# Layer 1 of a four-layer image network: VectorE in source order, small pieces between blocks, lengths after the values

## The chip, the core and the metric

The kernel runs on one core of a Trainium2 chip. The core has TensorE (PE, matrix products), VectorE (DVE), ScalarE (ACT), GpSimd (POOL) and SyncE (SP), which here issues the transfers. The metric is the device time of one execution in microseconds; the number quoted is the median of several executions.

## The reference

The input is 4 images of 56 x 56 positions (3136 tokens) with 256 channels, in 32-bit floats. Four layers follow each other, each adding its result to its input after a group normalisation. Only layer 1 is touched. For each image it computes:

```
xn = x / max(norm(x), 1e-12)                 # per token
A  = xn diag(W_adj) xn^T ; A = exp(5 (A - rowmax)) with a zero diagonal
A  = A / rowsum
y  = rowsum(A) * (x W_aff^T + b_aff) - (A x) W_aff^T
y  = LayerNorm(y) * gamma + beta ; y = max(y, 0.01 y)
```

x is the group-normalised input, and W_adj enters through its diagonal. The kernel applies W_aff first (the values xw = x W_aff^T), so one product A xw serves, and a column of -1 beside xw gives the row sums in the same product. A is symmetric before the division by the row sum, so a block of it computed once serves its rows and its columns.

## The kernel before

Layer 1 splits the 3136 tokens of an image into 24 tiles of 128 (NB) and a rest of 64 (REST). Tokens are loaded in chunks of four tiles: chunks 0 to 5 (NC4 is 6), and chunk 6 for the rest.

**Preparing tokens** (`tokens`, L1337). For a chunk there is a list of steps. `load` reads x (512 KB), normalises its two channel halves with the group statistics (L939, VectorE) and squares the result (L1355, ScalarE). `lengths` sums squares by TensorE products with a column of ones (L1363), limits them (L1365, VectorE), takes the power -1/2 (L1366, GpSimd) and spreads them on a diagonal (L1367, GpSimd). `values` multiplies two tiles by W_aff (L1376), copied out by ScalarE or VectorE (L954, L952). `unit_length` broadcasts the inverse lengths by a product with that diagonal (L1384) and multiplies (L1386, VectorE) into xnT.

**The loop over units.** A unit is a row tile j with up to four column tiles first to last (a block is one pair of tiles). `scaled` (L1401, GpSimd) multiplies row tile j by W_adj. `logits` (L1408) makes the products, ScalarE the exponentials (L1411), and on the diagonal GpSimd clears the main diagonal (L1413). `transposed` turns the blocks by TensorE (L1478) and ScalarE copies them (L1481). `products` then does for each column tile i a product by column into one of two PSUM buffers ps_v (L1497), which VectorE adds to acc in SBUF (`add_up`, L1420, or a first copy, L1423), and a product by row (L1492), summed in the PSUM buffer ps_o of tile j. The rest of 64 tokens has units of its own (`rest_logits`, `rest_transposed`, `rest_products`, L1459 and L1463), two of which for the next image stand after row tiles 20 and 21 of the image before, the third after row tile 0.

**Finishing a tile.** When row tile j has all its columns, `finish` (L1519) adds ps_o and acc (L1527), divides (L1531, L1533), takes mean and variance (L1536, L1537, L1538), their power -1/2 on GpSimd (L1540), normalises on VectorE (L1541), multiplies by gamma and adds beta on GpSimd (L1542, L1543) and takes the maximum on VectorE (L1544). It returns `add`, which transposes the tile back (L1549) and adds it to the residual xr (L1557); with all 448 tokens of a residual piece there, the statistics for layer 2 are taken (L894) and the piece is stored (L1561).

**The order of the work.** Two lists set it. `small` holds pairs of a due block count and a step; `small_step` runs one due step, twice in each unit: ahead of the transposes, and between the next unit's logits and the products. The steps of a chunk are due 8 blocks after its load, an add 6 blocks after its finish. `replace` starts a chunk of the next image at a certain row tile, once the current image no longer needs that chunk. `now` forces the steps of a chunk that a unit is about to read. The product order is written out like this because for layer 1 TensorE is fixed in source order (`run(1, ..., {E.PE}, ...)`). The instructions of the other engines and the transfers are put in order by a planner, which takes an instruction when its model says that it is ready, preferring earlier ones; the resulting order of each engine's queue is then static. Layers 0 and 2 are left to the planner wholly.

Of the kernel before, what the change touches and what calls it, by code (L numbers as in the profile page):

```python
# [35 lines left out]
P = 128  # L36
# [4 lines left out]
NCH = 7  # L41
# [789 lines left out]
def direct_blocks(ctx: ExitStack, tc: tile.TileContext, d: dict, watch):  # L831
# [488 lines left out]
    def layer1(early, big, pool, late, next_layer):  # L1320
# [16 lines left out]
        def tokens(b, c, ps_a=ps_m):  # L1337
# [6 lines left out]
            def load():  # L1344
                x = early.tile([P, CC, 512], FP, tag="x", name="x1")
# [5 lines left out]
                x1 = box["x"] = early.tile([P, CC, 512], FP, tag="xn", name="xn1")  # L1351
                sq = box["sq"] = x
                for h in range(CC):
                    normalise(x1[:, h, :n], x[:, h, :n], known(1, b), h)
                nc.scalar.activation(sq[:, :, :n], x1[:, :, :n], AF.Square)  # L1355

            def lengths():
                pm, sq = ps_a(), box["sq"]
# [33 lines left out]
            return [load, lengths] + [lambda i=i: values(i) for i in range(0, m, 2)] + [unit_length]  # L1392
# [23 lines left out]
        touched = set()  # L1416
# [36 lines left out]
        def rest_products(b, q, e, own, at):  # L1453
            po = psum_tile("o", 2)
            for i in range(4):
# [6 lines left out]
                for a in range(2):  # L1462
                    nc.tensor.matmul(po[a * REST:(a + 1) * REST, :C + 1], lhsT=at[:, i * P + a * REST:i * P + (a + 1) * REST],  # L1463
                                     rhs=xw[:, 8 * q + 4 * a + i, :], start=(i == 0), stop=(i == 3 and (a == 1 or own is None)))
            if own is not None:
# [18 lines left out]
        def products(b, j, first, last, e, at):  # L1484
# [18 lines left out]
            for n, i in enumerate(others):  # L1503
                by_column(i)
                if n:
                    by_row(rows.pop(0))
            for i in rows:
# [4 lines left out]
        def residual(b, c):  # L1512

            if (b, c) not in xr and c < NCH:
                xr[b, c] = late.tile([P, CC, CH], FP, tag="xr", name="xr1", bufs=3)
# [3 lines left out]
        def finish(b, j):  # L1519

            n = P if j < NB else REST
            y = late.tile([P, C + 1], FP, tag="y", name="y", bufs=5) if j < NB else y_rest
# [12 lines left out]
            mv = pool.tile([P, 2], FP, tag="mv", name="mv1")  # L1535
# [3 lines left out]
            rstd = pool.tile([P, 1], FP, tag="rstd", name="rstd")  # L1539
            nc.gpsimd.tensor_tensor(rstd[:n], mv[:n, 1:2], mhalf[:n, 0:1], ALU.pow)  # L1540
            nc.vector.tensor_scalar(y, y, mv[:n, 0:1], rstd[:n], ALU.subtract, ALU.mult)  # L1541
            nc.gpsimd.tensor_tensor(y, y, gamma[:n], ALU.mult)  # L1542
            nc.gpsimd.tensor_tensor(y, y, beta[:n], ALU.add)  # L1543
            nc.vector.scalar_tensor_tensor(y, y, 0.01, y, ALU.mult, ALU.max)  # L1544

            def add():
# [5 lines left out]
                while t0 < j * P + n:  # L1552
# [9 lines left out]
                    t0 = t1  # L1562
            return add
# [16 lines left out]
        for c in range(2):  # L1580
            fresh[c].pop(0)()
        for c in range(NC4 + 1):
            for step in fresh[c]:
                step()
            if c + 2 <= NC4:
                fresh[c + 2].pop(0)()
        small, done = [], 0

# [610 lines left out]
```

## Time and profile before

| | |
|---|---|
| runs shown | 4041.41, 4027.03, 4025.71 us, median 4027.03 |
| profiled execution | 4042.54 us, of which the span from first to last instruction is 4040.7 |
| TensorE busy | 3848.9 us (95%) |
| VectorE, ScalarE, GpSimd busy | 2356.6 (58%), 1381.2 (34%), 1746.3 us (43%) |
| mean granted TensorE clock | 0.974 |
| layer 1 on TensorE | from 811.0 us (first L1363) to 2813.4 us (last L1492) |

Line numbers are those of the kernel before. A stretch such as 860:2815 is in us from the start of the span. Busy time of TensorE alone doesn't tell a full clock from a half one; the column PEclk does. A wait is put down to the instruction that released it, by engine, tile and line.

### The profile page before, as it was taken

Reading aid. Unit: us, or ns where it says so; the run is one execution under the profiler, and the core shown is the slowest. Engines: PE = TensorE matmul, PEld = TensorE weight load, DVE = VectorE, ACT = ScalarE, POOL = GpSimd, SP = SyncE. Lnnn points to the kernel's source line nnn. Section 1 sums busy time; section 2 is a strip of 40 time slices with the busy share of each in tenths; the row PEclk is TensorE's granted clock in tenths of the full one; section 3 lists DMA queues with packets and bytes.
Section 4 is the critical chain, followed back from the end, with each engine's and each line's share of the span. In section 5 each row is a group of like instructions: output and inputs, shape, how many; then the busy total and the mean of one; then the engine's idle time right before and its main releaser. Section 6 shows DMA issues by size and latency. Waiting matters only on the chain.

```text
span 4040.7 us, 92344 instructions
## 1 busy us (share of the span) xinstructions
PE 3848.9 (95%) x38871; PEld 2716.9 (67%) x38871; DVE 2356.6 (58%) x4431; ACT 1381.2 (34%) x2927; POOL 1746.3 (43%) x1883
## 2 busy tenths in 40 slices
PE   7999999899999999999999999999999999899998
PEld 4566666566777667776777757776676766566665
DVE  6777777734444434444344443445687887666765
ACT  3444545422222222222222212221555555344443
POOL 3566667721123311233112321124677777555555
PEclk9999999999999999999999999999999999999999
DMA  8443333320000100001000000001344443434443
GB/s 270 108 131 109 111 117 105 96 102 6 19 23 20 40 6 15 24 24 31 6 19 19 29 19 1 19 10 37 105 127 126 124 127 114 151 118 128 134 127 94
DMA packets 268659, 301.84 MB, mean 75 GB/s; under 512 B 25926, under 2 KB 260584, under 8 KB 267752
## 3 DMA queue, kind: packets, MB, share of 16 engines
q1 hardware_dynamic: 267946, 295.76, 23.8%
q8 instruction: 308, 5.05, 0.5%
q14 instruction: 117, 0.96, 0.1%
q10 hardware_dynamic: 288, 0.08, 0.0%
HBM read 203.39 MB, written 92.37 MB: 73 GB/s over the span
## 4 chain that ended last, share of the span: by engine, by line
PE 48%; DVE 4%; POOL 2%; issue 1%; DMA 0%; ACT 0%; POOLq 0%; DVEq 0%; SPq 0%; ACTq 0%
PE ps_m L945 13%; PE ps_o L1492 6%; PE ps_s L1408 6%; PE ps_v L1497 6%; PE ps_m L971 4%; PE ps_o L1087 3%; PE ps_s L1058 3%; PE ps_o L1027 2%; PE ps_t L1478 1%; PE ps_s L1012 1%; DVE rs L1783 1%; PE ps_m L1376 1%; PE ps_m L1363 0%; DVE e L1065 0%; DVE rs L2017 0%
## 5 line engine op out<-in xcount | busy, mean ns | idle before, releaser
L1420 DVE TENSOR_TENSOR acc<-acc,ps_v 128x257 f32<-128x257 f32 x1104 | 455.6, 421 | 686.2 <-PE ps_v L1497 671.5
L1497 PE MATMUL ps_v<-xw,e 128*128 128x257 f32 x2208 | 613.1, 382 | 19.7 <-DVE acc L1420 18.1
L1492 PE MATMUL ps_o<-xw,at 128*128 128x257 f32 x2208 | 609.0, 379 | 0.0
L1408 PE MATMUL ps_s<-xnT,xd 128*128 128x512 f32 (+3 forms) x1344 | 571.1, 547 | 0.0
L1481 ACT COPY at<-ps_t 128x512 f32<-128x512 f32 (+3 forms) x332 | 170.8, 515 | 1050.4 <-PE ps_t L1478 1050.4
L1497 PEld LDWEIGHTS ps_v<-xw,e 128*128 128x128 f32 x2208 | 408.6, 189 | 171.1 <-issue 80.4
L1078 POOL TENSOR_TENSOR b<-e 126x336 f32<-126x336 f32 (+5 forms) x512 | 499.5, 996 | 8.4 <-ACT e L1066 0.3
L1492 PEld LDWEIGHTS ps_o<-xw,at 128*128 128x128 f32 x2208 | 419.1, 190 | 60.1
L945 PE MATMUL ps_m<-xn,w_wqkv 128*128 128x392 f32 x1024 | 383.0, 508 | 5.6 <-DVE vt L975 4.2
L1401 POOL TENSOR_SCALAR xd<-xnT,vec 128x128 f32<-128x128 f32 x192 | 115.0, 611 | 631.9 <-PE ps_s L1408 629.4
L1069 POOL TENSOR_TENSOR e<-e,m0t 126x672 f32<-126x672 f32 (+3 forms) x128 | 238.7, 1865 | 277.2 <-ACT e L1068 264.3
L1069 POOL TENSOR_TENSOR e<-e,bias 119x784 f32<-119x784 f32 (+5 forms) x128 | 244.4, 1910 | 179.4 <-ACT e L1068 178.2
L1408 PEld LDWEIGHTS ps_s<-xnT,xd 128*128 128x128 f32 x1344 | 225.5, 191 | 134.8 <-issue 126.2
L1411 ACT ACTIVATE e<-ps_s 128x512 f32<-128x512 f32 x336 | 185.4, 552 | 335.1 <-PE ps_s L1408 335.1
L990 ACT ACTIVATE no<-rs 128x168 f32<-128x168 f32 (+2 forms) x256 | 93.8, 367 | 597.4 <-DVE rs L1783 273.8
L945 PEld LDWEIGHTS ps_m<-xn,w_wqkv 128*128 128x128 f32 x1024 | 190.4, 193 | 130.5 <-ACT pr L2039 17.9
L1087 PEld LDWEIGHTS ps_o<-e,vp 124*32 124x32 f32 (+3 forms) x8192 | 177.5, 111 | 143.3 <-issue 99.3
L1087 PE MATMUL ps_o<-e,vp 124*32 124x112 f32 (+3 forms) x8192 | 241.3, 254 | 6.2 <-POOL e L1069 4.4
L1066 ACT ACTIVATE e<-e 126x672 f32<-126x672 f32 (+5 forms) x256 | 219.5, 857 | 20.4 <-DVE e L1065 7.7
L939 DVE TENSOR_SCALAR xn<-x,gst 128x28 f32<-128x28 f32 (+4 forms) x368 | 204.5, 609 | 33.1 <-PE ps_m L945 29.0
L1783 DVE RECIPROCAL rs<-ps_o 128x196 f32<-128x196 f32 (+2 forms) x128 | 176.0, 1375 | 80.9 <-PE ps_o L1087 80.0
L1019 POOL TENSOR_TENSOR e<-e,m3l 98x784 f32<-98x784 f32 x64 | 118.3, 1849 | 219.5 <-ACT e L1016 219.5
(196 smaller groups left out, 6337.3 us busy)
## 6 DMA issues: line engine op xcount, KB each, us to landing
x<-xr SPq DMA_DIRECT2D x64, 392.0 KB
x<-in_x SPq DMA_DIRECT2D x53, 448.0 KB
x<-x SPq DMA_DIRECT2D x60, 392.0 KB
xr<-x SPq DMA_DIRECT2D x60, 392.0 KB
vd<-v SPq DMA_DIRECT2D x72, 256.0 KB
xr<-in_x SPq DMA_DIRECT2D x32, 392.0 KB
xr<-x SPq DMA_DIRECT2D x28, 448.0 KB
x<-xr SPq DMA_DIRECT2D x28, 448.0 KB
```

The costliest lines, as they stand in the source:

```text
L939: nc.vector.tensor_scalar(dst, src, gst[:, h, 0:1], gst[:, h, 1:2], ALU.subtract, ALU.mult)
L945: nc.tensor.matmul(pm[:, :n], lhsT=w[:, h, col:col + P], rhs=rhs(h), start=(h == 0), stop=(h == CC - 1))
L1066: nc.scalar.activation(ev, ev, AF.Exp)
L1069: nc.gpsimd.tensor_tensor(parts(ev), parts(ev), w["emask"], ALU.mult)
L1078: nc.gpsimd.tensor_tensor(w["b"][a][:nk, :, :2 * nq].rearrange("p h (i c) -> p h i c", i=2), ev[:, :, :, 0, :], ev[:, :, :, 1, :], ALU.add)
L1087: nc.tensor.matmul(w["o"](k, i)[j * HD:(j + 1) * HD], lhsT=ones[:nk, :HD] if k else v(j, u), rhs=w["b"][j // 2][:nk, j % 2, i * nq:(i + 1) ...
L1408: nc.tensor.matmul(s[:, :n], lhsT=xd[j][:, h, :], rhs=xnT[:, h, first * P:last * P], start=(h == 0), stop=(h == CC - 1))
L1411: nc.scalar.activation(e[:, :n], s[:, :n], AF.Exp, scale=5.0)
L1420: nc.vector.tensor_tensor(acc[:, i, :], acc[:, i, :], pv[:, :C + 1], ALU.add)
L1492: nc.tensor.matmul(out[j][:, :C + 1], lhsT=e[:, col(i)] if i == j else at[:, col(i)], rhs=xw[:, i, :], start=(i == j), stop=(i == NB - 1))
L1497: nc.tensor.matmul(pv[:, :C + 1], lhsT=e[:, col(i)], rhs=xw[:, j, :], start=True, stop=True)
L1783: nc.vector.reciprocal(rs.rearrange("p (t c) -> p t c", t=2), pv[:, :, 1, :])
```

## The change

VectorE joins TensorE in source order for layer 1. To make that order usable, the work between the adds is cut into pieces:

- `tick` is called after each column of `products` and after each step of `rest_products`. It runs one piece: the first of `due` whose tick number has come, or else the first of `ticks`.
- `finish` keeps its VectorE instructions up to L1538 and the power on GpSimd at once; `normal` (L1541, L1542, L1543) is due 2 ticks later and `leaky` (L1544) 5 ticks later. `leaky` puts `add` into `small`, due 3 blocks later, with the mark -1. The adds of the rest tile follow that of tile 23 in one step.
- `settle` forces pieces and adds of older tiles ahead of the reuse of a y buffer or a residual buffer.
- `load` only starts the transfer; the two halves of the normalisation are pieces in `ticks`, after four empty ones, and `ready` forces them if a step needs them first.
- In a chunk the first `values` comes ahead of `lengths`, and the steps are due 12 blocks after the load instead of 8. The row tiles at which chunks 3, 4 and 5 are loaded move from 18, 20, 22 to 16, 19, 23.
- At the start of the layer the normalisation of chunk c+1 stands ahead of the steps of chunk c.
- mv and rstd have 7 buffers each.

The diff, with headers and file names left out:

```diff
...
             box = {}
 
             def load():
-                x = early.tile([P, CC, 512], FP, tag="x", name="x1")
+                x = box["x0"] = early.tile([P, CC, 512], FP, tag="x", name="x1")
                 if c < NC4:
                     nc.sync.dma_start(out=x[:, :, :n], in_=tokens_of(1, b, 4 * c * P, n))
                 else:
                     for i in range(2):
                         nc.sync.dma_start(out=x[:, :, i * REST:(i + 1) * REST], in_=tokens_of(1, b, NB * P, REST))
-                x1 = box["x"] = early.tile([P, CC, 512], FP, tag="xn", name="xn1")
-                sq = box["sq"] = x
-                for h in range(CC):
-                    normalise(x1[:, h, :n], x[:, h, :n], known(1, b), h)
-                nc.scalar.activation(sq[:, :, :n], x1[:, :, :n], AF.Square)
+                box["x"] = early.tile([P, CC, 512], FP, tag="xn", name="xn1")
+
+            def normal(h):
+                normalise(box["x"][:, h, :n], box["x0"][:, h, :n], known(1, b), h)
+                if h:
+                    nc.scalar.activation(box["x0"][:, :, :n], box["x"][:, :, :n], AF.Square)
 
             def lengths():
-                pm, sq = ps_a(), box["sq"]
+                pm, sq = ps_a(), box["x0"]
...
                     for h in range(CC):
                         nc.gpsimd.tensor_scalar_mul(xdr[:, h, :], xnT[:, h, NB * P:], adj[:, h:h + 1])
 
-            return [load, lengths] + [lambda i=i: values(i) for i in range(0, m, 2)] + [unit_length]
+            return [load], [lambda h=h: normal(h) for h in range(CC)], [lambda: values(0), lengths] + [lambda i=i: values(i) for i in range(2, m, 2)] + [unit_length]
 
         xd, out, xr = {}, {}, {}
         y_rest = late.tile([REST, C + 1], FP, name="yr", bufs=1)
...
                 nc.gpsimd.tensor_tensor(e[:, :P], e[:, :P], offd, ALU.mult)
             return e
 
-        touched = set()
+        touched, open_tiles = set(), []
+        ticks, due = [], []
+        ticked = 0
+
+        def settle(tile):
+
+            while open_tiles and open_tiles[0] <= tile:
+                add = next((a for a in small if a[2] == -1), None)
+                if add:
+                    small.remove(add)
+                    add[1]()
+                else:
+                    due.pop(0)[1]()
+
+        def tick():
+            nonlocal ticked
+            ticked += 1
+            if due and due[0][0] <= ticked:
+                due.pop(0)[1]()
+            elif ticks:
+                ticks.pop(0)()
 
         def add_up(b, i, pv, copy=nc.vector.tensor_copy):
             if (b, i) in touched:
...
                 for a in range(2):
                     nc.tensor.matmul(po[a * REST:(a + 1) * REST, :C + 1], lhsT=at[:, i * P + a * REST:i * P + (a + 1) * REST],
                                      rhs=xw[:, 8 * q + 4 * a + i, :], start=(i == 0), stop=(i == 3 and (a == 1 or own is None)))
+                tick()
             if own is not None:
                 nc.tensor.matmul(po[:REST, :C + 1], lhsT=own, rhs=xw[:REST, NB, :], start=False, stop=True)
             if q == 0:
...
                 by_column(i)
                 if n:
                     by_row(rows.pop(0))
+                tick()
             for i in rows:
                 by_row(i)
 
...
         def residual(b, c):
 
             if (b, c) not in xr and c < NCH:
+                if NCH * b + c >= 3:
+                    b3, c3 = divmod(NCH * b + c - 3, NCH)
+                    settle((b3, min(((c3 + 1) * CH - 1) // P, NB - 1)))
                 xr[b, c] = late.tile([P, CC, CH], FP, tag="xr", name="xr1", bufs=3)
                 nc.sync.dma_start(out=xr[b, c], in_=tokens_of(1, b, c * CH, CH))
             return xr.get((b, c))
...
         def finish(b, j):
 
             n = P if j < NB else REST
+            if j < NB:
+                if len(open_tiles) > 4:
+                    settle(open_tiles[-5])
+                open_tiles.append((b, j))
             y = late.tile([P, C + 1], FP, tag="y", name="y", bufs=5) if j < NB else y_rest
             u = pool.tile([P, C], FP, tag="u", name="u")
             rd = pool.tile([P, 1], FP, tag="rd", name="rd")
...
             y = y[:n, :C]
             nc.vector.scalar_tensor_tensor(y, y, rd[:n], u[:n], ALU.mult, ALU.add)
             st = pool.tile([P, 6], FP, tag="st", name="st1")
-            mv = pool.tile([P, 2], FP, tag="mv", name="mv1")
+            mv = pool.tile([P, 2], FP, tag="mv", name="mv1", bufs=7)
             nc.vector.bn_stats(out=st[:n], in_=y)
             nc.vector.bn_aggr(out=mv[:n], in_=st[:n])
             nc.vector.tensor_scalar_add(mv[:n, 1:2], mv[:n, 1:2], LN_EPS)
-            rstd = pool.tile([P, 1], FP, tag="rstd", name="rstd")
+            rstd = pool.tile([P, 1], FP, tag="rstd", name="rstd", bufs=7)
             nc.gpsimd.tensor_tensor(rstd[:n], mv[:n, 1:2], mhalf[:n, 0:1], ALU.pow)
-            nc.vector.tensor_scalar(y, y, mv[:n, 0:1], rstd[:n], ALU.subtract, ALU.mult)
-            nc.gpsimd.tensor_tensor(y, y, gamma[:n], ALU.mult)
-            nc.gpsimd.tensor_tensor(y, y, beta[:n], ALU.add)
-            nc.vector.scalar_tensor_tensor(y, y, 0.01, y, ALU.mult, ALU.max)
+
+            def normal():
+                nc.vector.tensor_scalar(y, y, mv[:n, 0:1], rstd[:n], ALU.subtract, ALU.mult)
+                nc.gpsimd.tensor_tensor(y, y, gamma[:n], ALU.mult)
+                nc.gpsimd.tensor_tensor(y, y, beta[:n], ALU.add)
+
+            def leaky():
+                nc.vector.scalar_tensor_tensor(y, y, 0.01, y, ALU.mult, ALU.max)
+                if j < NB:
+                    small.append((done + 3, add, -1))
 
             def add():
                 pt = ps_m()
...
                         add_stats(2, b, c, x)
                         nc.sync.dma_start(out=tokens_of(2, b, c * CH, CH), in_=x)
                     t0 = t1
+                if j < NB:
+                    open_tiles.remove((b, j))
+                if j == NB - 1:
+                    last_add()
+            due.extend([(ticked + 2, normal), (ticked + 5, leaky)])
+            due.sort(key=lambda a: a[0])
             return add
 
 
...
         turn = iter(range(6 * (NC4 + 1)))
         fresh = [tokens(0, c, lambda: psum_tile(*(("v", 2), ("o", 2), ("t", 1), ("s", 2))[next(turn) % 4])) for c in range(NC4 + 1)]
         for c in range(2):
-            fresh[c].pop(0)()
+            fresh[c][0].pop()()
+        for step in fresh[0][1]:
+            step()
         for c in range(NC4 + 1):
-            for step in fresh[c]:
+            for step in (fresh[c + 1][1] if c < NC4 else []) + fresh[c][2]:
                 step()
             if c + 2 <= NC4:
-                fresh[c + 2].pop(0)()
+                fresh[c + 2][0].pop()()
         small, done = [], 0
 
+        normals = {}
+
+        def ready(chunk):
+            for step in normals.pop(chunk, []):
+                if step in ticks:
+                    ticks.remove(step)
+                    step()
+
         def small_step():
-            for i, (when, step, _) in enumerate(small):
+            for i, (when, step, chunk) in enumerate(small):
                 if when <= done:
                     small.pop(i)
+                    if chunk and chunk != -1:
+                        ready(chunk)
                     return step()
             step_stats()
 
         def now(chunk):
 
+            ready(chunk)
             for item in [a for a in small if a[2] == chunk]:
                 small.remove(item)
                 item[1]()
 
         def replace(b, c):
             if b < NIMG:
-                for item in [a[2] for a in small if a[2]]:
+                for item in [a[2] for a in small if a[2] not in (None, -1)]:
                     now(item)
-                load, *steps = tokens(b, c)
+                (load,), normals[b, c], steps = tokens(b, c)
                 load()
-                small[:0] = [(done + 8, step, (b, c)) for step in steps]
+                ticks.extend([no_step] * 4 + normals[b, c])
+                small[:0] = [(done + 12, step, (b, c)) for step in steps]
 
         def begin(w):
             if w[1] is None:
...
             now((w[0], (w[3] - 1) // 4))
             return logits(*w)
 
+        begin_at = {3: NC4, 6: 0, 10: 1, 14: 2, 16: 3, 19: 4, 23: 5}
         e = begin(units[0])
         for k, w in enumerate(units):
             b, j, first = w[:3]
             if first == j:
                 residual(b, j * P // CH)
                 residual(b, j * P // CH + 1)
-                if j in (3, 6, 10, 14, 18, 20, 22):
-                    replace(b + 1, {3: NC4, 20: 4, 22: 5}.get(j, j // 4 - 1))
+                if j in begin_at:
+                    replace(b + 1, begin_at[j])
                 if (b, j) == (NIMG - 2, 8):
                     small += [(done + 20, step, None) for step in next_layer()]
             small_step()
...
                 products(*w, e, at)
                 done += w[3] - first
                 if w[3] == NB:
-                    adds = [finish(b, j)] + ([last_add] if j == NB - 1 else [])
-                    small += [(done + 6, add, None) for add in adds]
+                    finish(b, j)
             e = ahead
+        while ticks or due:
+            tick()
         return [step for _, step, _ in small]
 
 
...
     with pool_of(2, 0) as early, ExitStack() as ends:
         late = ends.enter_context(pool_of(1, 3))
         held = {}
-        last_steps = run(1, lambda own: layer1(*own, late, lambda: layer2_ahead(early, held)), {E.PE}, range(3))
+        last_steps = run(1, lambda own: layer1(*own, late, lambda: layer2_ahead(early, held)), {E.PE, E.DVE}, range(3))
         run(2, lambda own: layer2(held, *own, last_steps), None, range(1, 4))
     run(3, lambda own: layer3(*own), {E.PE, E.DVE, E.Activation, E.Pool}, range(4))
```

## The prediction

> **What bounds it now.** I began with the busy times of the page, then cut the span into stretches with the granted TensorE clock.
>
> ```profile
> PE 3848.9 (95%) x38871; PEld 2716.9 (67%) x38871; DVE 2356.6 (58%) x4431; ACT 1381.2 (34%) x2927; POOL 1746.3 (43%) x1883
> ```
>
> ```profile
> 1832.00:1932.00 100.00, 91.96 (x413) 58.23 (x412) 45.64 (x123) 19.07 (x38) 27.79 (x44) 0.91 0.08 26
> ...
> 1460.00:1790.00 330.00, 329.31 (x1458) 247.23 (x1458) 142.92 (x369) 72.06 (x131) 74.01 (x115) 1.00 0.06 18
> 810.00:860.00 50.00, 42.81 (x220) 34.63 (x220) 21.56 (x41) 14.83 (x20) 20.25 (x24) 0.94 0.56 206
> 860.00:2815.00 1955.00, 1908.51 (x8456) 1383.42 (x8453) 855.20 (x2251) 410.70 (x769) 467.12 (x731) 0.99 0.06 18
> ```
>
> Columns after the stretch: its length, busy us of PE, PEld, DVE, ACT, POOL, then PEclk, DMA share, GB/s. TensorE bounds layer 1: inside an image (1460 to 1790) it idles 0.7 us in 330. Where one image passes into the next (1832 to 1932) it idles 8 us in 100, at clock 0.91. From 860 to 2815 it idles 46.5 us: that, and the clock, is all that can be won. TensorE's waits in that stretch say on whom:
>
> ```profile
> PE ps_v L1497 <- DVE acc L1420: 18.1, 25, 1.5
> PE ps_v L1459 <- DVE acc L1423: 11.7, 9, 1.6
> PE ps_v L1459 <- DVE acc L1420: 8.5, 8, 2.1
> PE ps_m L1384 <- POOL rstd L1540: 3.0, 3, 1.0
> PE ps_v L1497 <- DVE mv L1538: 1.7, 4, 0.4
> ```
>
> These are 43.0 us: products waiting for one of the two ps_v buffers that VectorE empties by add_up. VectorE's own waits there, and one spot (start us, us, instruction, idle before and releaser), say why it is late though only 44% busy (855.2 of 1955):
>
> ```profile
> DVE y L1544 <- POOL y L1543: 124.4, 93, 2.1
> DVE y L1541 <- POOL rstd L1540: 61.2, 78, 1.6
> ```
>
> ```profile
> 1834.31 0.15 DVE L1538 TENSOR_SCALAR mv<-mv 128x1 f32<-128x1 f32 x1
> 1836.06 0.53 DVE L1541 TENSOR_SCALAR y<-y,mv,rstd 128x256 f32<-128x256 f32 x1 [1.59 <-POOL rstd L1540]
> 1836.51 0.41 DVE L1423 COPY acc<-ps_v 128x257 f32<-128x257 f32 x1
> 1838.24 0.42 DVE L1544 SCALAR_TENSOR_TENSOR y<-y 128x256 f32<-128x256 f32 x1 [1.31 <-POOL y L1543]
> ```
>
> ```profile
> 1836.98 0.70 PE L1459 MATMUL ps_v<-xw,e 64*128 64x257 f32 x4 [1.60 <-DVE acc L1423]
> 1837.61 0.92 PE L1463 MATMUL ps_o<-xw,at 128*64 128x257 f32 x4
> 1839.05 1.23 PE L1459 MATMUL ps_v<-xw,e 64*128 64x257 f32 x4 [0.52 <-DVE acc L1423]
> 1840.21 1.13 PE L1463 MATMUL ps_o<-xw,at 128*64 128x257 f32 x4
> ```
>
> finish's normalisation (L1541) stands in VectorE's queue ahead of the copy that frees ps_v, and waits 1.59 us for GpSimd's rstd; TensorE then idles 1.60 us. Soon after, the same four matmuls take 1.23 us instead of 0.70: the half clock.
>
> [...] 1840 to 1850 was granted 0.50, but after a stall of 1.60 us, [...] among 64-row matmuls.
>
> **The change, part by part.**
>
> (a) *finish in pieces.* Nothing is added: each tile keeps its VectorE work (0.43+0.16+0.49+0.43+0.18+0.15 = 1.83 us up to L1538, then L1541 0.43 and L1544 0.44). Only the place moves: L1541 two ticks after finish, L1544 three later. A tick is one column: add_up instructions come 0.87 us apart (0.42 busy, 0.45 idle), so a piece of 0.44 fits the idle. Between finish and the next column TensorE has transposes (about 0.43) and logits (1.72), which hide the 1.83 us block. rstd needs GpSimd's L1540 (0.57), or 1.6 us where two L1401 (1.2) go first; two ticks and the unit's start give over 3 us. L1542 and L1543 need 2 x 0.73 = 1.46 us plus latency; three ticks give 2.6 us. So waits on GpSimd should leave the queue. If that cover fails, each late piece holds the adds behind it, and these hold TensorE.
>
> (b) *Rest products* (64-row): each step is 1.28 us of TensorE against two adds (0.84) or one (0.42), plus a piece. Their 20.2 us of waits (11.7+8.5) should shrink to about 1.1 us an image, mainly where unit_length's multiply (1.2 us, L1386) stands just before them. The 1497 waits (19.8) include about 0.35 us behind most unit_length steps in mid-image; these stay, 1.4 us an image.
>
> (c) *New waits.* I followed the loop. Chunk 5 is loaded at block 23 instead of 22; with twelve blocks behind, its unit_length is forced in begin just ahead of the logits that read it. Price: ps_m (one buffer) waits for the values copy, about 0.55, then L1386's 1.22 plus latency stands bare, 1.45: 2.0 us an image, in place of the forced step at block 20 (the 3.0 us of L1384). The adds of tile 23 and the rest now share one step, with the statistics (2 x 0.6): 0.7 for ps_m and 0.85 for the late add_up, 1.55 us an image. Short units near block 20: 1.0 us an image.
> After: (1.4+1.1+2.0+1.55+1.0) x 3 image changes = 21, and 1 for the last image: 22 us against 44 (the 43.0 and 1.2 of smaller waits). Gain **22 us**.
>
> (d) *Clock.* The three 100 us image changes were granted 0.95, 0.91, 0.91: 23 us of clock missing at most. Where stalls of 1.6 to 2.1 us in rest products go, the dips after them may go; the first image's rest products at 870 to 880 ran unstalled at clock 1.00. But new waits of 2 us arise, and other executions may have had fewer dips. I take a third: **7 us**; ends 0 and 21.
>
> (e) *Start-up* (810 to 860, 7.2 us idle). values(0) before lengths leaves only values(2), 1.75 us, over the chain lengths, L1365, L1366, L1367, 2.65 us where GpSimd is free (812.72 to 815.27 and the handover): 0.9 us for each of six chunks, 1.2 more where L1401 goes between: 6.6 us. Against it, the wait of 3.4 us for chunk 4 (normalised at 837.17, behind unit_length of chunk 3) mostly goes, since x of c+1 is now normalised ahead. Loss **3 us**. In order, normalise of c+1 stands before L1365 of c: if x is late (DMA share is near 1.0 from 820 to 830) the chain waits; ends -2 and 8.
>
> (f) *End.* Four finishes drain in order: after finish(23), pieces of tiles 21 to 23 wait on GpSimd (6 x 0.73 = 4.4 us). Layer 2's first normalise came at 2816.1; if it must follow that drain it comes at about 2821.8: 0 to 5.7 us lost. I take **2**.
>
> (g) Nothing: ready, settle (my walk finds no settle forced), more mv and rstd buffers, SP loads. One 512 KB load per chunk stays, moved two blocks earlier (chunk 3), one earlier (4) or later (5); the queue's DMA share is 0.06. What holds a load is the x buffer, released by L1363, now four blocks later and still ahead of its use. Behind it on SP are residual loads and stores (448 KB), needed many units later; stores of an image's last residual go earlier. Cover lost, one load costs a few us.
>
> Sum on the profiled execution: 4042.5 - 22 - 7 + 3 + 2 = 4018.5 (span 4016.7). It stands 15.5 us above the median of the three runs, 4027.03; the same difference of -24 gives **4003 us**.
>
> **Rivals.**
>
> *Even trade.* The stalls move rather than go: queue order brings 35 us where I count 22, no dip goes, start-up costs 8 and the end 6: -9+14 = +5, about 4030. For it: 329.3 of 330 us busy mid-image shows that the old order is already perfect there, and a fixed order can only equal it. Against: the spot at 1836 is one of plain order.
>
> *Slower: a piece waits for GpSimd in every tile.* GpSimd and ScalarE are not in source order. If L1401 (1.2 us), L1413 (0.46) or L1366 goes between L1541 and L1543, the answer comes after 1.46+1.2+0.46 = 3.1 us instead of 1.5; past the three ticks (2.6) and the ps_v slack (0.2 us) TensorE stands. 0.6 us in each of 96 tiles is 58 us, less 22: 4063. It decides from 0.4 us a tile. Against: a unit boundary, 2.2 us more, usually lies between.
>
> *All goes.* Both stalls (44) and dips (21), start-up even: 4027-62 = 3965.
>
> **How the numbers follow.** Chances: mine 0.44, even trade 0.28, slower 0.20, all 0.08. About 0.5% (20 us) is what a measurement of this kernel can tell from no change, so faster means under 4007, slower over 4047. Mine at 4003 has its own range of 3985 to 4018 and falls partly within 0.5%, the even trade wholly. Faster 0.08 + about 0.40 of mine = 0.48; within 0.5%: 0.04 + 0.26 = 0.30; slower 0.20 + 0.02 = 0.22. The range reaches below to half of the larger gain and above over the start of the slower case: 3978 to 4052.
>
> **What would show it.** Right: waits of L1541 and L1544 on GpSimd fall from 186 us to under 30; ps_v waits of TensorE under 20 us; clock of the image changes above 0.95; a wait of about 1.5 us at L1408 on L1386 once an image. Wrong: L1420 waiting on TensorE less while TensorE waits inside images; start-up longer by over 8 us; a gap over 8 us before L971.

## The result, and the profile after

The median is 3979.95 us (3978.63 to 3992.22), against 4030.27 us (4025.71 to 4041.41) for the kernel before in the same comparison. The ratio is 0.9882, with a 95% interval of 0.9861 to 0.9902: 50 us, or 1.2%, faster. The forecast was 4003 us, with a range of 3978 to 4052: the sign was right and the gain about half of what came. The result lies 2 us inside the lower end of that range, and 5 us below the 3985 to 4018 that the main case had for itself.

The profiled execution took 3979.57 us (span 3977.7). Line numbers from here on are those of the kernel after, which names the same code as follows: the add 1441 (before 1420), the copy that frees ps_v 1444 (1423), products by column and by row 1519 and 1514 (1497, 1492), the same for the rest 1480 and 1484 (1459, 1463), normal 1573 to 1575 (1541 to 1543), leaky 1578 (1544), the rstd power 1570 (1540), an add's transposes and sum 1585 and 1593 (1549, 1557), unit_length 1385 and 1387 (1384, 1386), logits 1409 (1408), values 1377 (1376), the products of lengths 1364 (1363) and their diagonal 1368 (1367). The page's line of busy times:

```profile
PE 3816.3 (96%) x38871; PEld 2712.4 (68%) x38871; DVE 2367.7 (60%) x4431; ACT 1378.9 (35%) x2927; POOL 1745.9 (44%) x1883
```

The instruction counts are unchanged on every engine. TensorE is busy 32.6 us less with the same 38871 matmuls; over the whole span the clock records show 142.9 us at half speed instead of 212.9. The table cuts both profiles at four events on TensorE: the last matmul of layer 0, the first rest logits of layer 1, the last product by row of layer 1, and the first matmul of layer 2 (line 971). "Half clock" is the time within a stage in which the clock records show half speed; an unbroken stretch of it is called a dip. The third column is another execution of the kernel before, taken to see what chance does.

| us | before | before again | after |
|---|---|---|---|
| profiled execution | 4042.54 | 4023.54 | 3979.57 |
| to the end of layer 0 | 811.2 | 800.5 | 800.8 |
| half clock in layer 0 | 99 | 75 | 68 |
| start-up of layer 1, to the first rest logits | 47.8 | 47.8 | 54.9 |
| main part of layer 1 | 1954.4 | 1951.3 | 1898.0 |
| ... TensorE busy in it | 1909.5 | 1906.5 | 1886.7 |
| ... TensorE idle in it | 44.9 | 44.9 | 11.3 |
| ... half clock in it | 57.3 | 50.4 | 12.9 |
| to layer 2's first matmul | 3.7 | 3.7 | 3.1 |
| layers 2 and 3 | 1223.6 | 1218.4 | 1220.8 |

From profile to profile 63.0 us went: 10.3 in layer 0 (811.18 to 800.85), 2.8 in layers 2 and 3, both of which the change leaves alone, and -7.1 + 56.4 + 0.6 = 49.9 in layer 1. The 10.3 are chance: the same order of matmuls had 99 us of half clock once and 68 and 75 in the two other executions. So layer 1 alone accounts for the 50 us between the medians: idle time -33.6, busy time -22.8, start-up +7.1, end -0.6.

The stretches of the kernel after (length, busy us of PE, PEld, DVE, ACT, POOL, then PEclk, DMA share, GB/s), an image change, the middle of an image and the main part:

```profile
1824.00:1924.00 100.00, 97.25 (x447) 66.83 (x446) 48.49 (x128) 20.67 (x39) 23.89 (x39) 1.00 0.08 24
...
1450.00:1780.00 330.00, 329.55 (x1463) 249.02 (x1462) 144.63 (x370) 72.65 (x134) 75.25 (x117) 1.00 0.06 18
...
857.00:2755.00 1898.00, 1885.46 (x8455) 1383.41 (x8451) 867.09 (x2255) 410.41 (x770) 467.51 (x732) 1.00 0.06 18
```

The image change went from 91.96 us busy at clock 0.91 to 97.25 at 1.00. The middle of an image was full before and is full still. What TensorE still waits for, in layer 1 after its start-up (waiting tile, releaser, then us in total, times, longest):

```profile
PE ps_s L1409 <- DVE xnT L1387: 3.9, 3, 1.3
...
PE ps_m L1585 <- DVE xr L1593: 1.5, 3, 0.5
...
PE ps_m L1385 <- DVE xw L952: 1.3, 3, 0.4
PE ps_v L1519 <- DVE acc L1441: 1.2, 3, 0.4
```

Of the 43.0 us of the five lines shown before, 1.2 are left, and no wait in the rest products (1480). At their head now stands a wait for unit_length, once for each image change. VectorE's own waits for GpSimd in finish, 186 us before, are down to one line; line 1578 no longer appears among them:

```profile
DVE y L1573 <- POOL rstd L1570: 3.6, 5, 0.8
```

The spot among the rest products where the prediction showed 1.60 us of idle TensorE, now first as VectorE and then as TensorE saw it (start us, us, instruction, idle before and releaser):

```profile
1828.38 0.43 DVE L1444 COPY acc<-ps_v 128x257 f32<-128x257 f32 x1 [0.29 <-PE ps_v L1480]
1828.72 0.41 DVE L1573 TENSOR_SCALAR y<-y,mv,rstd 128x256 f32<-128x256 f32 x1
1830.09 0.42 DVE L1444 COPY acc<-ps_v 128x257 f32<-128x257 f32 x1 [0.97 <-PE ps_v L1480]
```

```profile
1826.42 0.70 PE L1480 MATMUL ps_v<-xw,e 64*128 64x257 f32 x4
1827.06 0.66 PE L1484 MATMUL ps_o<-xw,at 128*64 128x257 f32 x4
...
1829.36 0.70 PE L1480 MATMUL ps_v<-xw,e 64*128 64x257 f32 x4
```

The normalisation stands behind the copy, starts at once, and VectorE then idles 0.97 us for TensorE: the roles have changed. The four rest matmuls take 0.70 us, where they took 1.23 after the stall.

The start-up is what became longer. TensorE at the handover from layer 0:

```profile
795.60 5.25 PE L945 MATMUL ps_m<-attn,w_wo 128*128 128x392 f32 x8 [2.57 <-DVE attn L1239]
...
802.76 2.87 PE L1377 MATMUL ps_v<-w_waff,xn 128*128 128x256 f32 x8 [1.91 <-DVE xn L939]
...
805.42 3.41 PE L1364 MATMUL ps_o<-ones,x 128*128 128x1 f32 x16
```

and VectorE there:

```profile
801.55 0.57 DVE L894 BATCH_NORM_STATS2 st<-xr 128x6 f32<-128x392 f32 x1
...
802.19 0.52 DVE L939 TENSOR_SCALAR xn<-x,gst 128x512 f32<-128x512 f32 x1
```

In source order the first normalisation of layer 1 (939) stands behind the last statistics of layer 0 (894), so TensorE waits 1.91 us. Before, the planner put that normalisation 5.8 us ahead of the end of layer 0 at 811.2, and TensorE went on without a gap:

```profile
805.38 0.45 DVE L939 TENSOR_SCALAR xn<-x,gst 128x512 f32<-128x512 f32 x1
```

```profile
811.02 1.84 PE L1363 MATMUL ps_v<-ones,x 128*128 128x1 f32 x16
812.72 1.97 PE L1376 MATMUL ps_o<-w_waff,xn 128*128 128x256 f32 x8
```

After the gap the values and lengths take 2.87 and 3.41 us instead of 1.97 and 1.84: half clock, 11.0 us of it in the start-up against 4.2.

### The profile page after: what moved, and what is told of

It reads as the page before. It is cut to its first block, busy times and chain, and to the rows that moved or that the text cites. A ratio compares the mean times of both kernels' runs of the same rounds, so it can differ in the third digit from the quotient of the medians.

```text
span 3977.7 us, 92350 instructions
## 1 busy us (share of the span) xinstructions
PE 3816.3 (96%) x38871; PEld 2712.4 (68%) x38871; DVE 2367.7 (60%) x4431; ACT 1378.9 (35%) x2927; POOL 1745.9 (44%) x1883
## 5 line engine op out<-in xcount | busy, mean ns | idle before, releaser
L971 PE MATMUL ps_m<-w_wqkv,xn 128*128 128x256 f32 (+1 forms) x800 | 206.0, 396 | 9.4 <-DVE xr L1876 6.0
```

The source lines that it names most:

```text
L971: nc.tensor.matmul(pm[:k, j * C:(j + 1) * C], lhsT=xn[:, h, first:first + k], rhs=w[:, h, :], start=(h == 0), stop=(h == CC - 1))
```

## The experiments

All stand beside runs of the kernel before on the same chip. The table has the stages of each, in us; times are medians of 4 to 7 runs where a ratio stands, else one time. The other columns are of one profiled execution each.

| kernel | time | ratio (95%) | start-up | main | idle | half clock in main |
|---|---|---|---|---|---|---|
| before again | 4023.54 | | 47.8 | 1951.3 | 44.9 | 50.4 |
| after | 3979.95 | 0.9882 (0.9861-0.9902) | 54.9 | 1898.0 | 11.3 | 12.9 |
| pieces, VectorE planned | 4053.54 | 1.005 (1.003-1.007) | 54.3 | 1965.4 | 55.1 | 50.8 |
| source order, no pieces | 4321.41 | | 53.2 | 2236.9 | 251.8 | 202.3 |
| stall in rest products | 4043.88 | | 55.1 | 1957.0 | 46.6 | 69.5 |
| stall in mid-image | 4004.09 | | 54.9 | 1921.3 | 33.1 | 9.4 |
| long stall in mid-image | 4032.78 | | 54.9 | 1954.9 | 49.5 | 46.9 |
| pieces after one and two ticks | 4069.48 | 1.0099 (1.0083-1.0114) | 55.0 | 1986.5 | 84.6 | 12.8 |
| lengths first | 3977.35 | 0.987 (0.9854-0.9887) | 53.2 | 1895.8 | 11.3 | 7.8 |
| chunk 5 earlier | 3976.23 | 0.986 (0.9843-0.9876) | 54.9 | 1891.6 | 7.1 | 9.3 |
| all three | 3972.05 | 0.9858 (0.9839-0.9877) | 56.3 | 1887.2 | 5.7 | 4.5 |
| all three, start-up planned | 3965.05 | 0.9837 (0.9824-0.9851) | 47.6 | 1887.0 | 5.8 | 3.0 |

### Which half of the change brings the gain

*Pieces, VectorE planned.* The kernel after, with VectorE given back to the planner:

```diff
-run(1, ..., {E.PE, E.DVE}, ...)
+run(1, ..., {E.PE}, ...)
```

> The changed kernel with VectorE given back to the planner (only TensorE in source order); all pieces, ticks and due counts stay. If the fixed order is what wins, the waits of L1573 and L1578 on GpSimd return (over 100 us of VectorE, against 4 in the changed kernel), TensorE waits over 35 us on ps_v and the time goes back to 4015 to 4035. If the later place of the pieces in the program is enough for the planner too, it stays at 3975 to 3995 with under 20 us of ps_v waits.

It is 0.5% slower than before. TensorE's largest waits in the main part:

```profile
PE ps_v L1519 <- DVE acc L1441: 24.7, 30, 1.7
PE ps_v L1480 <- DVE acc L1444: 14.0, 9, 2.3
PE ps_v L1480 <- DVE acc L1441: 6.9, 7, 1.6
```

These 45.6 us are the three ps_v waits of before again (38.2 there), although the pieces stand in the source where they stand in the kernel after. VectorE waits 65.8 us for rstd and 121.6 us for GpSimd's gamma and beta, as before. The start-up is 54.3 us here too, so a loss there can come without source order on VectorE. Layer 1 begins without a gap (first matmul at 800.8, end of layer 0 at 800.9), but products wait for the diagonal of the lengths (1368), 7.5 us against 2.5 before:

```profile
PE ps_s L1385 <- POOL dg L1368: 5.6, 6, 2.2
PE ps_t L1385 <- POOL dg L1368: 1.9, 1, 1.9
```

*Source order, no pieces.* The kernel before, with VectorE fixed in source order:

```diff
-run(1, ..., {E.PE}, ...)
+run(1, ..., {E.PE, E.DVE}, ...)
```

> The kernel before with VectorE in source order and nothing else. If the pieces are needed, each finish holds the queue for 1.83 + 0.7 + 0.43 + 1.7 + 0.44 = 5.1 us against about 3.9 us that TensorE has until its third product by column: about 1.8 us in each of 96 tiles, 170 us, a time near 4200. If order alone is the gain (a fixed order without pieces is no worse than the planner's), 4030 or below.

At 4321 us it takes about 290 us more than before, well over the 170 that I had expected. TensorE's two largest waits in the main part, with the line numbers of before:

```profile
PE ps_v L1497 <- DVE acc L1420: 194.5, 83, 5.3
PE ps_m L1384 <- DVE xw L952: 27.7, 9, 4.2
```

A whole finish in front of the next tile's adds holds TensorE up to 5.3 us. I had counted the stalls and not the clock: 251.8 us of idle time came with 202.3 us of half clock, and busy time rose from 1909.5 to 1985.1 us. So neither half is worth anything alone; the order and the pieces work only together. "Pieces" means here all of the change but the order; no run tells finish's pieces from those of the normalisation or from the later due counts.

*Before again.* The kernel before, unchanged.

> The kernel before once more, for its clock. If the half clock at the image changes belongs to the kernel, they are granted 0.91 to 0.96 again, as in the first profile; layer 0, the same program in both kernels on TensorE, is granted less half clock than in the first profile (99 us before layer 1; 61 to 75 in four other profiles), so that layer 1 starts 5 to 10 us earlier than 811.0. If the image changes run at 0.98 or more, the clock's share of the gain was chance.

Its idle time in the main part is the same to 0.1 us, and its start-up too. Its half clock is not: 50.4 us against 57.3 in the main part, 75 against 99 in layer 0. The three image changes were granted 0.95, 0.91 and 0.95 (0.95, 0.91 and 0.91 in the first profile), so the half clock there belongs to the kernel. Over all profiles taken, layer 0, whose matmul order no kernel here changes, had between 68 and 106 us of it.

### Do the stalls bring the half clock?

*Stall in rest products.* In the kernel after, `finish` of tiles 0, 20 and 21 does both pieces at once, so that VectorE waits for GpSimd ahead of rest products:

```diff
-            due.extend([(ticked + 2, normal), (ticked + 5, leaky)])
-            due.sort(key=lambda a: a[0])
+            if j in (0, 20, 21):
+                normal()
+                leaky()
+            else:
+                due.extend([(ticked + 2, normal), (ticked + 5, leaky)])
+                due.sort(key=lambda a: a[0])
```

> The changed kernel, but for tiles 0, 20 and 21 of each image, most of them just ahead of the 64-row rest products, normal and leaky run at once in finish. 12 stalls of about 2.2 us: 24 to 28 us of waits on ps_v. Theory that stalls in the rest products bring the half clock: the image changes fall from a clock of 0.98 to 1.00 to about 0.93 and lose some 15 to 20 us more, so about 4020 to 4030. Rival that the half clock there was chance of an execution: clock stays above 0.98, about 4005.

*Stall in mid-image.* The same edit for tiles 4, 8 and 12, which are followed by products of 128 rows.

> The same for tiles 4, 8 and 12, in the middle of an image, where all products use 128 rows. 12 stalls of about 1.9 us: 22 us of waits, about 4003. Theory that the half clock needs a stall among 64-row products: clock there stays 1.00. Rival that any stall of 1.6 us or more brings it: clock of the stretches with the stalls falls below 0.97 and the time is 4015 or more.

Both edits delay the same number of finishes. The first cost 64 us and the second 24 (each one time, against the median of after). TensorE at one of the stalls of the first:

```profile
1831.30 1.22 PE L1480 MATMUL ps_v<-xw,e 64*128 64x257 f32 x2 [3.07 <-DVE acc L1444]
1832.45 1.13 PE L1484 MATMUL ps_o<-xw,at 128*64 128x257 f32 x4
```

After 3.07 us of idle time the matmuls run at half clock: the same four products by row take 1.13 us instead of 0.66. Idle time rose by 35.3 us and busy time by 23.7 (1910.4 - 1886.7), with half clock from 12.9 to 69.5. Seven stalls of 2.4 to 3.1 us lie in rest products, and a dip follows each; others fall elsewhere (three of 2.91 us ahead of 1385, one of 5.6 us at an add of the last image). In the second, the longest wait for ps_v and the clock in mid-image:

```profile
PE ps_v L1519 <- DVE acc L1441: 22.9, 15, 1.8
```

```profile
1450.00:1780.00 330.00, 324.11 (x1436) 244.07 (x1435) 141.53 (x361) 69.45 (x128) 71.90 (x112) 1.00 0.06 18
```

Twelve stalls of up to 1.8 us, and the clock stays 1.00: the time rose by the idle time alone (33.1 - 11.3 = 21.8; busy +1.5). In the kernel before, seven stalls of 1.6 us lie in rest products, and half clock followed four of them. So at like length the two places differ; no run varied the kind of matmul alone. (The stalls of the first run are longer; the comparison is between those of 1.6 us before and those of 1.8 us here.)

*Long stall in mid-image.* The edit of tiles 4, 8 and 12, and three more statistics after `leaky`, whose results are not used, to lengthen the stall and see whether products of 128 rows stay free of half clock then too:

```diff
+                for _ in range(3):
+                    nc.vector.bn_stats(out=st[:n], in_=y)
```

> As the kernel with stalls behind tiles 4, 8 and 12, with three more statistics instructions (3 x 0.43 us, results unused) behind leaky there, so that each stall is about 3.1 us, as long as the longest among the rest products (3.07). 12 x 3.1 = 37 us of waits, about 4018. Theory that the half clock follows a stall's length alone: half clock behind most of the 12 stalls, another 10 to 25 us. [...]

Two of the twelve long stalls, without and with half clock after them:

```profile
1153.54 0.70 PE L1519 MATMUL ps_v<-xw,e 128*128 128x257 f32 x2 [3.19 <-DVE acc L1441]
1238.15 1.23 PE L1519 MATMUL ps_v<-xw,e 128*128 128x257 f32 x2 [3.19 <-DVE acc L1441]
```

Both waited 3.19 us for the same kind of product. Eight of the twelve stalls were followed by half clock, 37.5 us of it in all, and four were not. So among the same products half clock followed most of the stalls of 3.19 us and none of those of 1.8 us. What sets the eight apart from the four was not shown.

### The slower rival

*Pieces one and two ticks after finish.* `normal` due after one tick and `leaky` after two, so that GpSimd cannot be done in time:

```diff
-            due.extend([(ticked + 2, normal), (ticked + 5, leaky)])
+            due.extend([(ticked + 1, normal), (ticked + 2, leaky)])
```

> The changed kernel with normal due 1 tick after finish and leaky 2 (instead of 2 and 5). By the prediction's arithmetic (GpSimd needs 1.46 us and the handover, one tick is 0.87 us, the slack of ps_v 0.2 us) VectorE waits about 0.7 us for GpSimd in most of 96 tiles and TensorE about 0.5: 30 to 50 us, 4010 to 4030. If the three columns and the 2.2 us of transposes and logits behind the first unit of a row tile cover a late piece, VectorE's waits return but TensorE's do not: 3980 to 3990.

VectorE's largest wait for GpSimd, and TensorE's largest wait, in layer 1:

```profile
DVE y L1578 <- POOL y L1575: 113.5, 90, 1.5
```

```profile
PE ps_m L1585 <- DVE y L1578: 61.9, 70, 2.0
```

The rival's time came (4069 against its 4063), but by another path, so the agreement is luck; the 4010 to 4030 that I expected of this run was missed by 40 us. VectorE waits about 1.3 us in most tiles (113.5 / 90), as foreseen, but with two ps_v buffers little of that reaches the products by column: they wait 1.3 us in all at 1519 and 4.5 at 1480. What stops TensorE is the add, due three blocks after `leaky`: its transposes (1585) read y, and TensorE reaches them in its own fixed order before the late `leaky` has ended. The idle time rose by 73.3 us. The half clock did not rise (12.8): 60 of the 70 waits are of 0.7 to 0.9 us, and of the ten of 1.3 to 2.0 us one was followed by a dip, of 3.4 us from 2815.3 on, in which the logits (1409) took 3.31 us instead of 1.88:

```profile
2814.49 0.44 PE L1585 MATMUL ps_m<-ident,y 128*128 128x128 f32 x2 [1.94 <-DVE y L1578]
```

### The start-up and the waits that are left

*Lengths first.* In the start-up alone, the order of before (lengths ahead of the first values):

```diff
-            for step in ... + fresh[c][2]:
+            first, second, *others = fresh[c][2]
+            for step in ... + [second, first] + others:
```

> The changed kernel with lengths ahead of the first values again, at the start of the layer only. The six waits of L1385 on GpSimd there (2.2 + 4 x 0.69 + 1.9 = 6.9 us) fall to about 2, so the start gets about 5 us shorter and the time about 3975. If instead the loads or the normalisation ahead limit the start, waits of the same size appear at another product and the time stays at 3980.

The start-up fell by 1.7 us only. The six waits for the diagonal (1385 on 1368), 6.9 us in all after the change, fell to 4.6, and in place of the 1.91 us for the normalisation came 3.46 us for ScalarE's square behind it. The order of values and lengths is thus not the whole cause of the loss: with lengths first, 53.2 us are left in source order, where TensorE still begins late.

*Chunk 5 earlier.* Loaded at row tile 22 as before, without the four empty ticks, and due 9 blocks later instead of 12, so that its unit_length is not forced:

```diff
-... 19: 4, 23: 5}
+... 19: 4, 22: 5}
-ticks.extend([no_step] * 4 + normals[b, c])
+ticks.extend([no_step] * (0 if c == 5 else 4) + normals[b, c])
-small[:0] = [(done + 12, step, (b, c)) for step in steps]
+small[:0] = [(done + (9 if c == 5 else 12), step, (b, c)) for step in steps]
```

> The changed kernel with chunk 5 loaded at row tile 22, due 9 blocks later and normalised without the four empty pieces, so that its unit_length stands one unit ahead of the logits that read it. The waits of L1409 on xnT (3 x 1.31) and of L1385 on the values copy (3 x 0.44) go, 5.2 us: about 3975. If the adds that are pushed later (tiles 22 and 23) wait instead, the time stays at 3980.

As expected: the 1.3 us at the logits (1409) and the 0.4 at unit_length (1385) go at each image change, and idle time falls by 4.2 us, from 11.3 to 7.1.

*All three.* Both of these, and the adds of tile 23 and the rest in two steps:

```diff
-                if j == NB - 1:
-                    last_add()
+                if j == NB - 1 and b < NIMG - 1:
+                    small.append((done, last_add, None))
+                elif j == NB - 1:
+                    last_add()
```

> Both of these, and the add of the rest tile as a step of its own (removes the waits of L1585 on xr, 3 x 0.52, and of ps_v behind it, 3 x 0.40): sum 5 + 5 + 3 = 13 us, about 3967. If the parts overlap in what they win, 3972 to 3978.

Idle time falls to 5.7 us. Its main part is 10.8 us shorter than after's; its median is 7.9 us shorter, 5 us short of what I expected. Its profiled execution happened to have 106 us of half clock in layer 0 and 19.4 in the start-up, so the start-up's 56.3 is not to be compared.

*All three, start-up planned.* VectorE is fixed only from the loop over units on; in the start-up TensorE alone is:

```diff
+        startup = tc.manual_schedule(engines={PE})
+        startup.__enter__()
         ... start-up of the layer
+        startup.__exit__(None, None, None)
+        both = tc.manual_schedule(engines={PE, DVE})
+        both.__enter__()
         ... loop over units
+        both.__exit__(None, None, None)
```

> The kernel with all three edits, with the fixed order of VectorE beginning only after the start of the layer, whose VectorE instructions the planner places again. Theory that the start (from the end of layer 0 on TensorE to the first rest logits: 47.8 us before, 54.9 in the changed kernel) is longer because in source order the first normalisation of layer 1 stands behind the last VectorE work of layer 0: it moves ahead of it again, TensorE begins layer 1 without a wait, and the start is 46 to 49 us, so 3965 or below. If the loads or the order of lengths and values make it longer, it stays above 52 and the time at 3970 to 3973.

VectorE ahead of the end of layer 0 (799.5 us on TensorE):

```profile
793.62 0.45 DVE L939 TENSOR_SCALAR xn<-x,gst 128x512 f32<-128x512 f32 x1
793.98 0.38 DVE L1239 TENSOR_TENSOR attn<-ps_o,rs 128x224 f32<-128x224 f32 x1
```

The normalisation (939) is again taken between instructions of layer 0 (1239), and the start-up takes 47.6 us, as before the change. It has lengths first too, so four runs cross the two choices: 54.9 us with values first in source order, 54.3 with values first and planned, 53.2 with lengths first in source order, 47.6 with lengths first and planned. Either choice alone wins little; only both together win back the 7 us. The time is 3965.05 us, a ratio of 0.9837 with an interval that ends below the one of the kernel after: this version is faster than the kernel before and the kernel after.

## Why the prediction was right or wrong

**(a) Finish in pieces: right.** The waits of VectorE for GpSimd went from 186 to 3.6 us (five waits for rstd); two and five ticks are enough, and with one and two they come back (113.5 us).

**(b) Rest products: right.** The 20.2 us of waits for ps_v there are gone; I had left about 1.1 us an image. (I called all of the 43.0 us waits for ps_v; 3.0 of them, at L1384, were for ps_m.)

**(c) New waits: right in kind, too dear.** I left 22 us of idle time, and 11.3 were measured: a gain of 33.6 instead of 22. The forced unit_length of chunk 5 (loaded at row tile 23, which I called a block) was priced at 2.0 us an image, and the two lines show 1.3 + 0.4 = 1.7. The joint adds of tile 23 and the rest were priced at 1.55; the trace has about 0.9 (0.5 on the sum, 0.4 on ps_v). The terms that failed are the 1.4 us an image behind unit_length in mid-image and the 1.0 for short units: neither appears. I took the waits of 0.35 us behind unit_length for a price of its multiply; in the trace before, one of them, at 1100.68, came where halves of the next normalisation (939) stood between the adds that follow the multiply. After the change those are pieces of their own, one for each tick.

**(d) Clock: the sign right, the size wrong.** I took 7 us, with an upper end of 21; the busy time fell by 22.8 (19.8 against the second execution of before). Half clock in the main part fell by 44.4 us, so by my estimate a microsecond of it cost about half a microsecond of busy time here (22.8 / 44.4). I took a third on two grounds: "new waits of 2 us arise", but they lie among 128-row products, and the three that came (0.44 and 1.31 us close together, once an image) were followed by one dip, of 3.4 us; and "other executions may have had fewer dips", but the second one had 50.4 us against 57.3. Of the 12.9 us that remain, 9.5 belong to a dip that began as the start-up ended.

**(e) Start-up: the sign right, the size at its upper end, a term missing.** +7.1 against +3. The two terms that I priced came: the waits for the diagonal grew from 2.5 to 6.9 us (+4.4, where I had 6.6), and the wait of 3.4 us for chunk 4 went. I passed over the handover: the first normalisation, which the planner had hoisted into layer 0, now waits behind layer 0's last statistics. That is 1.9 us of wait, and with 6.8 us more half clock the start-up's busy time rose by 4.3 (40.6 to 44.9). The crossed runs agree that there are two causes: planned, but with values first, there was no gap at the handover and the start-up was 6.5 us longer, 5.0 of it waits for the diagonal; in source order, but with lengths first, it was 5.4 us longer. Together they cost 7.1 and not their sum; the waits for a later chunk's normalisation (3.4 us before, 3.6 with pieces and VectorE planned), which only source order removed, are a part of the difference.

**(f) End: wrong in sign, small.** -0.6 against +2. The gap before layer 2's first matmul is 3.1 us; layer 2 belongs to the planner, and its first normalisation does not wait for the drain of the last pieces.

**(g) Nothing: right.** No wait for a transfer of layer 1 appears among the largest, and the mid-image stretch is as full as before (329.55 of 330 us).

The sum was -22 - 7 + 3 + 2 = -24, and layer 1 gave -33.6 - 22.8 + 7.1 - 0.6 = -49.9. All the errors but that of the start-up lie on one side, so the forecast was right in its direction and about half in size. Of the rivals, "all goes" (3965, given 0.08) was nearest for stalls and clock; the start-up kept the time above it, and the version with all three edits and the start-up planned came to 3965 too, which is luck: its own terms, 44 and 21, make 65 and 3962. The even trade fell with (c) and (d). The slower one was shown to be real but not in this kernel: at two and five ticks hardly a piece is late. Its 0.6 us a tile does not follow from its numbers either: 3.1 less 2.6 and 0.2 is 0.3, which gives about 4034 and not 4063.

## What to carry to other kernels

A queue's order is worth as much as its work: with the same number of VectorE instructions (4431) the kernel took 4321, 4054 or 3980 us. When an engine that is only 44% busy makes another wait, look at what stands ahead of the instruction that frees the buffer; cut the work that waits for a third engine into pieces with its latency between them, and fix the order only where the pieces are, leaving the handover from the stage before to whatever hoists work across it. Price a stall with the clock that follows it: here 33.6 us less idle time came with 22.8 us less busy time, so a microsecond of stall cost about two thirds as much again (22.8 / 33.6, an estimate); stalls of 1.8 us in mid-image cost next to nothing more (1.5 us for twelve).

## What the runs showed of the hardware

**Stalls of like length were followed by half clock in one place and not in another.** The table counts the stalls of five groups, by the matmuls around them. Half clock shows in the matmuls themselves: in the stall shown in rest products, four products by row took 1.13 us instead of 0.66.

| stalls | among | followed by half clock |
|---|---|---|
| 10 of 1.6 to 2.1 us (before) | 64-row rest products | 7 of 10 |
| 7 of 2.4 to 3.1 us (stall in rest products) | 64-row rest products | 7 of 7 |
| 12 of 1.8 us (stall in mid-image) | 128-row products | none |
| 10 of 1.3 to 2.0 us (pieces after one and two ticks) | transposes and 128-row products | 1 of 10 |
| 12 of 3.19 us (long stall in mid-image) | 128-row products | 8 of 12 |

In the main part of layer 1 the dips lasted 3.4 to 13.7 us before, and after 3.4 and 10.2 us, of which the longer began in the start-up. So a stall of 1.6 us could be followed by more half clock than it lasted itself: from 1840 to 1850, behind the one at 1836.98 before, the granted clock was 0.50.

Length and place vary together over the groups, but for the two in mid-image: there, stalls of 1.8 us were followed by no half clock, and 8 of 12 stalls of 3.19 us were. In the rest products of the kernel before, stalls of 1.6 to 2.1 us were followed by it 7 times in 10. Why it followed some stalls and not others of the same length in the same place was not shown, and no run varied the rows of the matmuls alone.

**The half clock of layer 0 differed from execution to execution**: 99 and 75 us in two executions of the kernel before, and 68 to 106 us over the thirteen profiles, with the same matmul order; the end of layer 0 lay between 797.4 and 815.2 us. These 18 us are about 0.5% of the kernel's time, so two single profiles of it cannot be compared more closely than that as wholes, only stage by stage.
